# Pairwise bilinear products: the software queue's weight loads on 15 DMA engines instead of 14

## The chip, the cores and the metric

The kernel runs on one core of a Trainium2 chip. The metric is device time in microseconds (us). A core has five engines with an instruction stream each: TensorE (PE) multiplies matrices, VectorE (DVE), ScalarE (ACT) and GpSimd (POOL) work element by element, and SyncE (SP) issues transfers. Sixteen DMA engines move data between the chip's main memory (HBM) and the on-chip memory of 128 partitions. SyncE and ScalarE issue transfers on hardware queues, GpSimd on a software queue; all three queues run on the same sixteen DMA engines.

## The reference

There are 32 fields of 128 numbers for each of 1024 samples, and one 128 x 128 matrix for each of the 496 pairs (i, j) with i < j:

```python
v_i = inputs[:, I_IDX, :]
v_j = inputs[:, J_IDX, :]
transformed = jnp.einsum('bpd,ped->bpe', v_i, W)
return transformed * v_j
```

`inputs` is (1024, 32, 128), `W` is (496, 128, 128), all float32. The result, 1024 x 496 x 128 floats, is 260 MB; the inputs together are 49 MB.

## The kernel before

**Tiles.** The host lays x out as one 128 x 1024 tile for each field (embedding on the partitions, samples along the free dimension). The pairs are put in the order of falling i and numbered q = 0 to 495. The weights of eight pairs form one load of 128 partitions x 1024 floats, 512 KB. There are 62 such loads, c = 0 to 61. The output is stored transposed, in 124 tiles of four pairs (128 x 4 x 1024 floats, 2 MB each), and the host transposes back.

**Work per pair.** A step u handles half a pair, 512 samples. The first 15 pairs use one matmul a half (L237). All others split x and W into a rounded part and a rest, and use three matmuls a half: two in `first` (L240), which ScalarE then scales in place (L242), and one in `second` (L251), three steps later. VectorE multiplies the sum with the tile of field j into the output tile (L261). ScalarE rounds the weights (L142), GpSimd makes their rests (L144 to L146).

**Order.** The order of every engine's instructions is written out by the loop at the end of `tile_bilinear_pairs_kernel`. Stores go out on ScalarE's queue two steps after their last product: whole tiles of 2 MB, but tiles 72 to 80 (`HALF`) in halves of 1 MB, and the first and the last tile in smaller pieces. Output tiles rotate over three buffers and, where they are free, over the buffers of the grouped x tiles. VectorE's first product of a tile waits until the last store from its buffer has landed.

**Weight loads.** Three buffers hold weight loads. When the last split of a load is done, the loop takes the next one off `ring` and loads it into the buffer that came free, so a load is issued while the two before it in `ring` are still to be split. Loads with odd c, and the first ones, go out whole on SyncE's queue (L126). The 25 loads in `WAPART`, c = 12, 14 to 60, go out in two parts, in `load_apart`: the first `ROWS` = 8 x `NE` = 112 partitions on GpSimd's software queue (L108), the last 16 on SyncE's queue (L109). For these loads the host has reordered the first 112 rows, so that the source can be read as 14 groups (the slowest dimension, `a`) of 8 rows each; group a goes to the partitions 8a to 8a + 7.

**Marks.** After each such load, `BACK` = 3 pairs later, `move_on(2)` issues a small transfer on the software queue (L105). It writes a few rows of 64 bytes into a tile `mark` that nothing reads. With one `move_on(5)` at the first split pair (L283) and `move_on(13)` after the last load (L289), its arguments add up so that 14 + 2 = 16 for each load, and 5 + 25 x 14 + 24 x 2 + 13 = 416 = 26 x 16 for the whole kernel. The engines that a load leaves out are called spared below.

Of the kernel before, what the change touches and what calls it, by code (L numbers as in the profile page):

```python
# [30 lines left out]
XLEAD = 5  # L31

XG = 4
NE = 14
ROWS = 8 * NE
WAPART = tuple(range(12, 62, 2))
BACK = 3
# [14 lines left out]
def kernel(  # L52
# [22 lines left out]
    nc = tc.nc  # L75
# [12 lines left out]
    def load_x(f, pieces=1, eng=None):  # L88
        if f == 0:

            t = rpool.tile([P, WL, P], F32, tag="w", name="x_0").rearrange("p q e -> p (q e)")
        else:
            t = xpool.tile([P, BT], F32, tag=f"x{f}", name=f"x_{f}")
        s = BT // pieces
        for k in range(pieces):
            (eng or nc.sync).dma_start(out=t[:, k * s : (k + 1) * s], in_=xt[f, :, k * s : (k + 1) * s])
        x_sb[f] = t
# [3 lines left out]
    mark = xpool.tile([32, 16], F32, tag="mark", name="mark")  # L101

    def move_on(k):

        nc.gpsimd.dma_start(out=mark[: 2 * k], in_=xt[0, : 2 * k, :16].rearrange("(b a) n -> a b n", a=k))  # L105

    def load_apart(dst, src):
        nc.gpsimd.dma_start(out=dst[:ROWS], in_=src[:ROWS].rearrange("(b a) m n -> a b m n", a=NE))  # L108
        nc.sync.dma_start(out=dst[ROWS:], in_=src[ROWS:])  # L109
# [3 lines left out]
    def load_group(k, m):  # L113
        if m == XG - 1:
            group[k] = xpool.tile([P, XG, BT], F32, tag=f"g{k}", name=f"x_g{k}")
        f = XG * k + 1 + m
        x_sb[f] = group[k][:, m, :]
        nc.sync.dma_start(out=x_sb[f], in_=xt[f])

    def load_w(c, splits=(0, WL), eng=nc.sync):  # L120
        w_raw[c] = rpool.tile([P, WL, P], F32, tag="w", name=f"w_{c}")
        if c in WAPART:
            load_apart(w_raw[c], wt[c])
            return
        for a, b in zip(splits, splits[1:]):
            eng.dma_start(out=w_raw[c][:, a:b, :], in_=wt[c, :, a:b, :])  # L126
# [102 lines left out]
    def first(u):  # L229
        q, h = divmod(u, 2)  # L230
        i, c = pairs[q][0], q // WC
        r = slice(q % WC * P, (q % WC + 1) * P)
        s = slice(h * HB, (h + 1) * HB)
        if h == 0:
            po[q] = ppool.tile([P, BT], F32, tag="po", name=f"po_{q}")
        if q < nq0:
            nc.tensor.matmul(po[q][:, s], w_raw[q // WL][:, q % WL, :], x_sb[i][:, s], start=True, stop=True)  # L237
        else:
            for t in (0, 1):
                m = nc.tensor.matmul(po[q][:, s], w_s[c][t][:, r], x_s[i][t][:, s], start=t == 0, stop=t == 1)  # L240
                apart(m, scaled.get(u - 1) if h else None)
            scaled[u] = nc.scalar.mul(po[q][:, s], po[q][:, s], 1.0 + EPS)  # L242
            apart(scaled[u], taken.get(q - PB), "TensorE's products, which this waits for, have waited for it")

    def second(u):
        q, h = divmod(u, 2)
        i, j = pairs[q]
        r = slice(q % WC * P, (q % WC + 1) * P)
        s = slice(h * HB, (h + 1) * HB)
        if q >= nq0:  # L250
            m = nc.tensor.matmul(  # L251
                po[q][:, s], w_s[q // WC][2][:, r], x_s[i][2][:, s], start=False, stop=True, skip_group_check=True
            )
            apart(m, scaled[u ^ 1])
        g, k = divmod(q, OG)
        if k == 0 and h == 0:
            ots[g] = out_tile(g)
        if q >= NQ - 2:
            nc.vector.tensor_tensor(ots[g][:, k, s], po[q][:, s], x_sb[j][:, s], ALU.mult)  # L259
        elif h == 1:  # L260
            taken[q] = nc.vector.tensor_tensor(ots[g][:, k, :], po.pop(q), x_sb[j], ALU.mult)  # L261
            if HALF[0] < g <= HALF[-1]:
                apart(taken[q], taken.get(q - 3 * OG), "one engine writes both, in order")
        if q >= NQ - 2:
            stores.append((u + SLAG, out[g, :, k, s], ots[g][:, k, s]))
        elif g == 0 or q >= NQ - OG:
            if h == 1:
                stores.append((u + SLAG, out[g, :, k], ots[g][:, k]))
        elif g in HALF:
            if k % 2 == 1 and h == 1:  # L270
                stores.append((u + SLAG, out[g, :, k - 1 : k + 1], ots[g][:, k - 1 : k + 1]))
        elif k == OG - 1 and h == 1:
            stores.append((u + SLAG, out[g], ots[g]))

    for u in range(2 * NQ + LAG + SLAG):
        q = u // 2
        if u < 2 * NQ:
            i, j = pairs[q]
            if u % 2 == 0 and j == i + 1 and XG * ngroup < i - 2 - XLEAD:
                load_x(i - 2 - XLEAD)  # L280
            first(u)
            if u == 2 * nq0:
                move_on(5)  # L283
            if u % 2 == 0 and q in group_at:
                load_group(*group_at[q])
            if u % 2 == 1 and q in w_at:
                load_w(w_at[q])
            if u % 2 == 0 and q in back:
                move_on(16 - NE if max(w_raw) < WAPART[-1] else 13)  # L289
        if LAG <= u < 2 * NQ + LAG:  # L290
            second(u - LAG)
        while stores and stores[0][0] <= u - LAG:
            nc.scalar.dma_start(*stores.pop(0)[1:])
        if u % 2 == 1:
            ready = [t for t in todo if t[0] <= q]
            if ready:
                ready[0][2](u)
                todo.remove(ready[0])
        if ring[WB:] and ring[0] in spent:
            ring.pop(0)  # L300
            c = ring[WB - 1]
            if c == "x":
                load_x(0)
            else:
                load_w(c)
            if c in WAPART:
                back.append(q + BACK)
        while later and later[0][0] <= u:
            nc.vector.tensor_tensor(*later.pop(0)[1:], ALU.subtract)  # L309
# [31 lines left out]
```

## Time and profile before

| | |
|---|---|
| Three timed runs | 746.7, 749.0 and 752.5 us, median 749.0 |
| Profiled execution | 747.5 us, its span 745.8 us, mean granted TensorE clock 0.99 |
| TensorE matmul, weight load | 704.2 us (94%), 548.9 us (74%) busy |
| VectorE, ScalarE, GpSimd | 635.6, 635.4 and 596.8 us busy (85, 85 and 80%) |
| HBM | 49.29 MB read, 260.05 MB written, 415 GB/s over the span |
| Stores of 2 MB | 113, 13.0 us from issue to landing in the median |
| Software queue's loads of 448 KB | 25, issued from 125.5 to 683.5 us, 625 ns of GpSimd each, 11.8 us to landing |
| SyncE's parts of 64 KB | 25, issued from 124.2 to 682.3 us, 6.0 us to landing |
| SyncE's loads of 512 KB of weights | 36, 11.1 us to landing |
| Marks | 26, issued from 31.2 to 686.2 us, 634 ns of GpSimd each in the median, 10.1 us to landing |

Busy time is the time that an engine's instructions cover; it does not tell which engine is waited for. The profile also gives DMA shares: the time that packets took, as a share of what the 16 engines have. As packets on one engine overlap by some nanoseconds, a share can be a little over 1. The chain that ended last, followed back from the last instruction, is put down to TensorE for 65% of the span, to transfers for 19%, to VectorE for 7% and to GpSimd for 5%.

### The profile page before, as it was taken

To read this page: it belongs to the slowest core of one execution; us is meant where nothing else is said; L and a number is where in the kernel's file an instruction comes from. 1 tells how busy PE (TensorE), PEld (TensorE's weight loads), DVE (VectorE), ACT (ScalarE), POOL (GpSimd) and SP (SyncE) were. 2 spreads that over 40 slices of the span, in tenths; PEclk is the share of its full clock that TensorE was granted. 3 is DMA by queue.
4 is the path that set the end of the run, shared out by engine and by line. 5 is a ranking of instruction groups with operands and counts; after the bars stand their busy time and mean duration, and the time that the engine had idled before them with its cause. 6 is when DMAs were issued, how large, how long until landed. Compare 5 with 4: busy or idle time off the path is not lost.

```text
span 745.8 us, 10667 instructions
## 1 busy us (share of the span) xinstructions
PE 704.2 (94%) x2946; PEld 548.9 (74%) x2946; DVE 635.6 (85%) x550; ACT 635.4 (85%) x1256; POOL 596.8 (80%) x882
## 2 busy tenths in 40 slices
PE   7999999999999999999899979988999999999994
PEld 3577777777878887786687758866878777777783
DVE  4888999999999998887789858978988888888884
ACT  1398999999999999898899959988989989988893
POOL 1789999999999999878778857977787878796660
PEclk9999999999999999999999989999999999999997
DMA  9999999999999999999999999999999999999998
GB/s 345 426 424 428 427 428 428 425 427 421 428 419 426 426 423 426 425 422 425 427 421 430 421 423 382 417 420 431 407 423 408 422 413 418 393 407 416 423 389 342
DMA packets 35963, 310.04 MB, mean 416 GB/s; under 512 B 5440, under 2 KB 5568, under 8 KB 19136
## 3 DMA queue, kind: packets, MB, share of 16 engines
q10 hardware_dynamic: 20880, 261.10, 83.4%
q1 hardware_dynamic: 10592, 36.77, 12.3%
q0 software_dynamic: 4432, 11.48, 4.0%
q8 instruction: 24, 0.39, 0.2%
q14 instruction: 35, 0.29, 0.1%
HBM read 49.29 MB, written 260.05 MB: 415 GB/s over the span
## 4 chain that ended last, share of the span: by engine, by line
PE 65%; DMA 19%; DVE 7%; POOL 5%; issue 2%; ACT 1%; SPq 0%; DVEq 0%; POOLq 0%; ACTq 0%
PE po L240 42%; PE po L251 20%; DMA out_dram<-ot 18%; DVE ot L261 5%; PE po L237 3%; DVE xd L309 2%; POOL wd L146 1%; POOL wl L144 1%; POOL xl L161 1%; DMA x<-in_xt_dram 1%; POOL xl L162 1%; POOL wd L145 0%; ACT po L242 0%; DVE ot L259 0%; ACT wh L142 0%
## 5 line engine op out<-in xcount | busy, mean ns | idle before, releaser
L242 ACT ACTIVATE po<-po 128x512 f32<-128x512 f32 x962 | 553.6, 584 | 78.1 <-PE po L240 63.8
L261 DVE TENSOR_TENSOR ot<-po,x 128x1024 f32<-128x1024 f32 x358 | 430.1, 1221 | 70.2 <-DMA out_dram<-ot 20.9
L240 PE MATMUL po<-xh,wh 128*128 128x512 f32 x962 | 382.5, 398 | 23.0 <-DVE ot L261 22.4
L251 PE MATMUL po<-xd,wd 128*128 128x512 f32 x962 | 376.0, 391 | 4.8 <-DVE xd L309 2.4
L240 PE MATMUL po<-xl,wl 128*128 128x512 f32 x962 | 377.0, 392 | 1.5 <-POOL wl L144 0.9
L240 PEld LDWEIGHTS po<-xh,wh 128*128 128x128 f32 x962 | 181.0, 188 | 82.0 <-DVE ot L261 45.3
L144 POOL TENSOR_TENSOR wl<-w,wh 128x256 fp32r<-128x256 f32 x241 | 184.4, 765 | 66.6 <-ACT wh L142 60.8
L251 PEld LDWEIGHTS po<-xd,wd 128*128 128x128 f32 x962 | 180.9, 188 | 45.4 <-DVE ot L259 3.2
L240 PEld LDWEIGHTS po<-xl,wl 128*128 128x128 f32 x962 | 181.2, 188 | 41.3 <-POOL wl L144 4.2
L146 POOL TENSOR_TENSOR wd<-wl,wd 128x256 fp32r<-128x256 f32 x241 | 181.8, 754 | 20.1
L261 DVE TENSOR_TENSOR ot<-po,x_g 128x1024 f32<-128x1024 f32 x136 | 164.0, 1223 | 31.3 <-DMA out_dram<-ot 11.4
L145 POOL TENSOR_SCALAR wd<-wh 128x256 fp32r<-128x256 f32 x241 | 104.0, 432 | 20.5
L142 ACT ACTIVATE wh<-w 128x256 fp32r<-128x256 f32 x241 | 98.6, 410 | 7.0 <-DVE ot L261 3.6
L309 DVE TENSOR_TENSOR xd<-xh,xl 128x512 fp32r<-128x512 f32 x52 | 46.8, 901 | 0.0
L161 POOL TENSOR_TENSOR xl<-x_g,xh 128x512 fp32r<-128x512 f32 x32 | 41.7, 1302 | 4.2 <-ACT xh L160 3.9
L161 POOL TENSOR_TENSOR xl<-x,xh 128x512 fp32r<-128x512 f32 x20 | 25.9, 1293 | 15.6 <-ACT xh L160 15.3
L162 POOL TENSOR_SCALAR xl<-xl 128x512 fp32r<-128x512 f32 x52 | 34.5, 664 | 4.6
L237 PE MATMUL po<-x,w 128*128 128x512 f32 x60 | 28.1, 624 | 4.1 <-DMA x<-in_xt_dram 3.9
L237 PEld LDWEIGHTS po<-x,w 128*128 128x128 f32 x60 | 11.6, 198 | 19.8 <-issue 13.6
L160 ACT ACTIVATE xh<-x 128x512 fp32r<-128x512 f32 x20 | 12.3, 624 | 11.3 <-DMA x<-in_xt_dram 11.2
L160 ACT ACTIVATE xh<-x_g 128x512 fp32r<-128x512 f32 x32 | 20.0, 624 | 0.0
L105 POOL DMA_DIRECT2D mark<-in_xt_dram x26 | 16.6, 639 | 0.0
(7 smaller groups left out, 20.0 us busy)
## 6 DMA issues: line engine op xcount, KB each, us to landing
out_dram<-ot ACTq DMA_DIRECT2D x113, 2048.0 KB, 13.0
w<-in_wt_dram SPq DMA_DIRECT2D x36, 512.0 KB, 11.1
out_dram<-ot ACTq DMA_DIRECT2D x18, 1024.0 KB, 11.8
w<-in_wt_dram POOLq DMA_DIRECT2D x25, 448.0 KB, 11.8
x_g<-in_xt_dram SPq DMA_DIRECT2D x16, 512.0 KB, 16.4
x<-in_xt_dram SPq DMA_DIRECT2D x14, 512.0 KB, 9.5
out_dram<-ot ACTq DMA_DIRECT2D x6, 512.0 KB, 8.5
w<-in_wt_dram SPq DMA_DIRECT2D x26, 64.0 KB, 6.0
```

The costliest lines, as they stand in the source:

```text
L142: halved[c] = nc.scalar.mul(h, raw, 1.0 - 2.0**-13)
L144: nc.gpsimd.tensor_tensor(l, raw, h.bitcast(F32), ALU.subtract)
L145: nc.gpsimd.tensor_scalar(d, h.bitcast(F32), EPS, 1.0, ALU.mult, ALU.mult)
L146: nc.gpsimd.tensor_tensor(d, l.bitcast(F32), d.bitcast(F32), ALU.subtract)
L161: nc.gpsimd.tensor_tensor(l, x_sb[f][:, s], h.bitcast(F32), ALU.subtract)
L162: nc.gpsimd.tensor_scalar(l, l.bitcast(F32), 1.0 / EPS, 1.0, ALU.mult, ALU.mult)
L237: nc.tensor.matmul(po[q][:, s], w_raw[q // WL][:, q % WL, :], x_sb[i][:, s], start=True, stop=True)
L240: m = nc.tensor.matmul(po[q][:, s], w_s[c][t][:, r], x_s[i][t][:, s], start=t == 0, stop=t == 1)
L242: scaled[u] = nc.scalar.mul(po[q][:, s], po[q][:, s], 1.0 + EPS)
L251: m = nc.tensor.matmul(po[q][:, s], w_s[q // WC][2][:, r], x_s[i][2][:, s], start=False, stop=True, skip_group_check=True)
L261: taken[q] = nc.vector.tensor_tensor(ots[g][:, k, :], po.pop(q), x_sb[j], ALU.mult)
L309: nc.vector.tensor_tensor(*later.pop(0)[1:], ALU.subtract)
```

## The change

`NE` goes from 14 to 15. So a load in `WAPART` puts 120 partitions on the software queue, from a source whose slowest dimension is 15, and 8 partitions on SyncE's queue; the host reorders 120 rows to match. The mark after each load is called with 16 - 15 = 1 and becomes a transfer of a single element; the first mark is called with 4, and the last one, as before, with 13: 4 + 25 x 15 + 24 x 1 + 13 = 416 again. The spread over the ring becomes 15 engines, with one left out, and that is the fourth from where the cursor stands at the kernel's start. The halves of tiles 72 to 80 are in both kernels and are not changed.

```diff
-NE = 14
+NE = 15
 ROWS = 8 * NE
...
     def move_on(k):
 
-        nc.gpsimd.dma_start(out=mark[: 2 * k], in_=xt[0, : 2 * k, :16].rearrange("(b a) n -> a b n", a=k))
+        if k == 1:
+            nc.gpsimd.dma_start(out=mark[:1, :1], in_=xt[0, :1, :1])
+        else:
+            nc.gpsimd.dma_start(out=mark[: 2 * k], in_=xt[0, : 2 * k, :16].rearrange("(b a) n -> a b n", a=k))
...
             if u == 2 * nq0:
-                move_on(5)
+                move_on(4)
```

## The prediction

> **What bounds the kernel now.** I read the DMA part of the page first, because one row of it has no free slice:
>
> ```profile
> DMA  9999999999999999999999999999999999999998
> DMA packets 35963, 310.04 MB, mean 416 GB/s; under 512 B 5440, under 2 KB 5568, under 8 KB 19136
> ...
> q10 hardware_dynamic: 20880, 261.10, 83.4%
> q1 hardware_dynamic: 10592, 36.77, 12.3%
> q0 software_dynamic: 4432, 11.48, 4.0%
> ```
>
> The reader is to see that the queues' shares sum to about 100% of 16 engines' span: the stores (q10) take 83.4, SyncE's loads (q1) 12.3, the software queue that the change touches (q0) only 4.0. The DMA engines have no rest. Next, the busy times by stretch (columns: stretch, length, each engine's busy us with its instructions, granted clock, DMA share, GB/s); the 25 loads in question are issued between 125.5 and 683.5 us:
>
> ```profile
> 125.00:694.00 569.00, 547.01 (x2338) 435.61 (x2338) 491.68 (x426) 509.95 (x1011) 475.84 (x710) 0.99 1.01 419
> ...
> 712.00:730.00 18.00, 18.00 (x81) 14.91 (x80) 16.24 (x14) 16.62 (x33) 11.73 (x19) 1.00 0.94 400
> ```
>
> From 712 us the DMA share falls under 1 and TensorE does 81 matmuls in 18 us, 4.5 per us. In the loads' stretch it does 2338 in 569, 4.11 per us. At 4.5 it would need 519 us, so it has some 50 us of slack there, though it looks 96% busy: the DMA engines set the pace. The waits show where that enters:
>
> ```profile
> PEld po L240 <- DVE ot L261: 45.3, 59, 5.8
> DVE ot L261 <- DMA out_dram<-ot: 32.3, 35, 6.2
> ...
> ACT wh L142 <- DMA w<-in_wt_dram: 1.3, 1, 1.3
> ```
>
> VectorE waits for an output tile whose store has not landed, TensorE's weight loads then wait for VectorE; the weights themselves are waited for once, 1.3 us.
>
> A store is over when the last of the 16 engines is, so what counts is the load of each engine, which no view gives. The trace has every packet's start, length, size and queue, not its engine. But a packet starts 3 to 4 ns before the one ahead of it on its engine ends, so 16 chains can be followed, closely enough through the first nine loads. From 40 to 315 us: every chain did 420 to 428 packets of stores (all keep step), with idle gaps of a few us at most. Fourteen chains moved 7.31 to 7.38 MB, and their packets took together about 1.0 us each more than the usual durations (611 ns for 16 KB, 159 ns for 4 KB). The two spared ones, which have no 4 KB packets of the software queue, moved 7.06 and 7.07 MB, and theirs took 10.9 and 11.1 us more. One is slow steadily: from about 40 us on, 16 KB take mostly 626 to 655 ns instead of 611. The other is slow in bursts of 650 to 1208 ns, from the time at which the loads begin. Sparing took 72 packets of 159 ns, 11.4 us, from each; slowness gave 10 back. **Both spared engines are slow, and sparing them is what makes all sixteen equal.**
>
> **What the Trainium skill says.** "DMA: Bandwidth & Descriptors", section "Why a DMA increments its semaphore by 16 and not by 1": the engine count k is the largest up to 16 that divides both sides' slowest dimension; the software queue takes k consecutive engines from a cursor that goes round, a hardware queue the lowest-numbered k. The trace agrees: 66 packets of 128 B, which is 5 + 24 x 2 + 13, the marks' values of k; two chains per load carry no data; and they stay the same two, so the marks do move the cursor. The same page, section "Latency and other measured facts", calls engines 7 and 15 usually slower. Here the two slow chains both carried data of the first mark, the one of five engines, so they lie among the first five of the ring: the trace decides. Section "Queues, rings and completion order": an engine goes round its queues packet by packet. The trace agrees: the 4 KB packets of a load come mostly every 0.76 us on an engine, 611 + 159 less the overlap.
>
> **The change, part by part.** TensorE, VectorE and ScalarE issue the same instructions in the same order. POOL and SyncE issue the same number at the same places; only their shapes differ.
> (a) The load on POOL (L108 before): 120 rows on 15 engines instead of 112 on 14. The first mark now moves the cursor by 4, and 15 engines from there leave out only the fourth. The fifth, spared before, gains 8 packets of 4 KB in each of 25 loads: 200 x 159 ns = 31.8 us. It loses the 8 fillers of 4 B that a spared engine gets in their place, 200 x 9 ns = 1.8. Net **+30.0 us on that one engine**. It has no free time to hide it in: its chain is full from 40 to 315 us, and the DMA share stays at 0.99 or more until 712. The bound from below is nothing, if its slowness went away; from above, 200 x 178 ns, the longer 4 KB packets that the steadily slow chain shows, 35.6 less 1.8, so 34.
> (b) SyncE's part (L109): 8 rows instead of 16. By the skill k is then 8, the first eight engines, one row each, as now. The last eight lose 25 x 159 ns = 4.0 us each. Worth nothing: the others do not get faster, and stores wait for the slowest.
> (c) The marks: the first of 8 rows instead of 10, 24 of one element instead of four rows. A mark takes POOL 634 ns before, and the trace has none of one element. Some 0.1 us either way each, 2.4 us in all, on an engine that is 80% busy and that nothing waits for but by short waits at L240 (4.2 us). I take 0.
> (d) What is queued behind: a load's 8 packets need 5.5 us on a chain (129.8 to 135.3 us in the first), so it is not held up by the stores' backlog on that engine, since the queues take turns. Stores are late, then VectorE at L261, then TensorE.
>
> Sum: +30.0, less what the engine can catch up where it is not full. From 712 to 730 us the share is 0.94, 1.1 us idle, and about 1 of the last 16 us: **+28**. Span 745.8 + 28 = 774; the profiled execution took 747.5, and the median of three is 749.0, 1.5 above it. Forecast **777 us**, plus 3.7%.
>
> **Rivals.**
> R1, not slower: the slowness leaves the engine, because it comes of being spared, of the fillers, of a full fabric, or of being traced. Then the fifth engine becomes one of 15 equal ones, 9 rows a load as they have, and the time stays at **748 to 749**. For it: the bursts begin only with the loads. Against it: the steady one is slow from 40 us, before any load, and the bursts also hit it (388 to 390 us: 993 ns on one and 979 on the other). The slowness is 10 us in 275, some 26 to 28 us over the run, and each us that stays is one of time: it decides where under 7.5 of them stay.
> R2, the change does not do what it says: a mark of one element does not move the cursor. Each load then starts one engine earlier in the ring, the spared place goes round, and both slow engines lose nearly all their relief: 30 us less the one or two loads in which each is spared, **775 to 779**. The trace shows k of 2, 5 and 13 moving the cursor, never 1.
> R3, more than the sum: the weights come late as well, and ScalarE's split (L142), with POOL behind it, waits at each load: 1 us at 25 loads, **800**. Against it: one wait of 1.3 us in the whole run, though SyncE's loads take 11.1 us to land in the median and POOL's 11.8.
>
> **How the numbers follow.** My forecast 0.79, R1 0.09, R2 0.06, R3 0.06. Own range of the forecast: 768 (a third of the slowness gone) to 783 (long packets, 749 + 34). For 8 in 10 I go down to 762, half the slowness gone, and up to 786; R1 and R3 stay out, 0.15. About 1% (7.5 us; the three runs differ by 5.7) is what can be told from no change. Slower by more: 0.79 + 0.06 + 0.06 less 0.01 for a forecast that shrinks under it, 0.90. Within: R1's larger part and that 0.01, 0.08. Faster: 0.02, the rest of R1.
>
> **What would show it.** Right: 3,000 packets of 4 KB on q0 instead of 2,800 and 200 fewer on q1; bytes nearly the same; the DMA share down from 1.01 to about 0.97 in the loads' stretch, since fifteen engines wait for one; stores some us longer to land than 13.0; VectorE's wait for them up from 32 us to perhaps 60; TensorE's 4.11 matmuls per us down to 3.9. Wrong: the share still 1.01 with the time unchanged (R1), data missing on a different engine at each load (R2), or ScalarE waiting for weights (R3).

## The result and the profile after

The changed kernel takes **758.7 us** in the median of four runs, beside 748.1 for the kernel before on the same chip: ratio 1.0132 [1.0089, 1.0175]. It is slower, by 10 us and not by the 28 forecast, and under the whole range of 762 to 786. The profiled execution took 759.2 us, its span 757.3, which is 11.5 more than before. Lines have moved down by 3: L261 is now L264, L240 is L243, L105 is L106 (one element) and L108 (other marks).

The DMA part of the page of the changed kernel (slices of the span; then packets; then queues with packets, MB, share):

```profile
DMA  9999999999999999899999997999999999999997
...
DMA packets 35563, 310.03 MB, mean 409 GB/s; under 512 B 5040, under 2 KB 5168, under 8 KB 18736
...
q10 hardware_dynamic: 20880, 261.10, 82.1%
q1 hardware_dynamic: 10192, 35.95, 12.1%
q0 software_dynamic: 4432, 12.30, 4.6%
```

The row of nines is almost the same, but for an 8 in the 17th slice and a 7 in the 25th: about 303 to 322 and 454 to 473 us. The bytes are the same and the rate fell from 416 to 409 GB/s. The busy times by stretch of the changed kernel (stretch, length, busy us with instructions of PE, PEld, DVE, ACT, POOL, then clock, DMA share, GB/s):

```profile
125.00:694.00 569.00, 541.94 (x2300) 429.38 (x2298) 483.86 (x420) 502.97 (x994) 468.58 (x700) 0.99 1.00 412
...
712.00:730.00 18.00, 18.00 (x80) 14.73 (x80) 16.11 (x14) 16.27 (x33) 11.97 (x19) 1.00 0.97 412
```

The DMA share in the loads' stretch is 1.00 where 0.97 was forecast, and TensorE does 2300 / 569 = 4.04 matmuls per us (4.11 before, 3.9 forecast). The waits of the changed kernel (us in total, times, longest):

```profile
PEld po L243 <- DVE ot L264: 52.8, 65, 6.1
DVE ot L264 <- DMA out_dram<-ot: 49.4, 45, 6.6
PE po L243 <- DVE ot L264: 26.9, 34, 5.7
```

It is the chain of the prediction: VectorE waits for a store to land, TensorE for VectorE. VectorE's wait grew by 17 us, that of TensorE's weight loads by 7.5. That of its matmuls grew by 4.5; before, it was:

```profile
PE po L240 <- DVE ot L261: 22.4, 26, 5.4
```

Now to where in the run. Busy times of two stretches, first of the kernel before, then of the changed one:

```profile
290.00:330.00 40.00, 38.22 (x166) 30.39 (x165) 33.78 (x30) 36.04 (x72) 33.32 (x51) 1.00 1.01 426
400.00:475.00 75.00, 69.48 (x293) 55.71 (x292) 60.85 (x54) 63.13 (x127) 57.95 (x88) 0.95 1.00 411
```

```profile
290.00:330.00 40.00, 34.86 (x145) 28.01 (x144) 30.26 (x27) 31.19 (x63) 27.87 (x42) 0.91 0.95 386
400.00:475.00 75.00, 68.62 (x283) 54.01 (x282) 58.18 (x52) 61.50 (x121) 55.41 (x84) 0.95 0.94 382
```

Here, and hardly elsewhere, the engines do stand idle: TensorE does 21 and 10 matmuls fewer. VectorE's timeline of the changed kernel at the first place (start, length, idle before it and what ended it):

```profile
296.98 1.22 DVE L264 TENSOR_TENSOR ot<-po,x 128x1024 f32<-128x1024 f32 x1
304.20 1.23 DVE L264 TENSOR_TENSOR ot<-po,x 128x1024 f32<-128x1024 f32 x1 [6.00 <-DMA out_dram<-ot]
```

One wait for a store, of 6 us. In the kernel before VectorE waits at most 1.7 us at a time between 290 and 330. These two places are where output tiles lose buffers: from pair 199 and from pair 293 on, at about 300 and 440 us, one that had been lent goes back to the grouped x tiles. (One also goes at pair 121, near 190 us, and no dip is seen there; the slow engine has little lag then.) So it looks as if a store can be late for a long time without cost, as long as there are buffers to spare, and the lateness is paid when they go.

**Whose stores are late.** With the packets put into 16 chains as in the prediction, between 40 and 300 us the steadily slow engine (the fifth of the ring) did 383 packets of the stores' queue, the others about 400. Some 15 of these 17 are 16 KB, 0.61 us each, so it lags by about 9 us. Eight loads' 8 packets of 159 ns come to 10.2. Nothing of this lag is in the DMA share.

**Where 11.5 us are, in packets.** All packets' lengths together, divided by 16 engines, are 746.05 us before and 750.15 after: 4.1 us of longer packets (the loads' 4 KB went from 163 to 169 ns in the mean, while those of 16 KB stayed, 617 and 616 ns between 40 and 300 us). Of these 4.1 us, 1.2 lie between 40 and 125 us, before the first of the 25 loads; why they are longer there is not known. Time without a packet, in the mean of the engines, was 7.6 us before and 14.9 after: 7.3 more, of which 2.4 at 300 to 320 us and 4.7 at 440 to 480. 4.1 + 7.3 = 11.4 us.

### The profile page after: what moved, and what is told of

Same layout as the page of the kernel before. It is cut to its first block, busy times and chain, and to the rows that moved or that the text cites. A ratio compares the mean times of both kernels' runs of the same rounds, so it can differ in the third digit from the quotient of the medians.

```text
span 757.3 us, 10667 instructions
## 1 busy us (share of the span) xinstructions
PE 710.3 (94%) x2946; PEld 550.9 (73%) x2946; DVE 635.2 (84%) x550; ACT 636.6 (84%) x1256; POOL 595.6 (79%) x882
## 4 chain that ended last, share of the span: by engine, by line
PE 50%; DMA 32%; DVE 8%; POOL 4%; issue 3%; ACT 1%; DVEq 0%; ACTq 0%; POOLq 0%
PE po L243 32%; DMA out_dram<-ot 31%; PE po L254 15%; DVE ot L264 6%; PE po L240 4%; DVE xd L312 2%; POOL wd L149 1%; POOL wl L147 1%; ACT po L245 1%; POOL xl L164 1%; DMA x<-in_xt_dram 1%; ACT wh L145 0%; POOL wd L148 0%; DVE ot L262 0%; POOL xl L165 0%
## 5 line engine op out<-in xcount | busy, mean ns | idle before, releaser
L264 DVE TENSOR_TENSOR ot<-po,x 128x1024 f32<-128x1024 f32 x358 | 429.6, 1221 | 81.7 <-DMA out_dram<-ot 32.0
L243 PE MATMUL po<-xh,wh 128*128 128x512 f32 x962 | 384.5, 400 | 28.1 <-DVE ot L264 26.9
L243 PE MATMUL po<-xl,wl 128*128 128x512 f32 x962 | 378.1, 393 | 1.3 <-POOL wl L147 1.0
L243 PEld LDWEIGHTS po<-xh,wh 128*128 128x128 f32 x962 | 181.6, 189 | 89.8 <-DVE ot L264 52.8
L243 PEld LDWEIGHTS po<-xl,wl 128*128 128x128 f32 x962 | 181.9, 189 | 40.6 <-POOL wl L147 3.9
L264 DVE TENSOR_TENSOR ot<-po,x_g 128x1024 f32<-128x1024 f32 x136 | 163.3, 1222 | 31.1 <-DMA out_dram<-ot 17.3
L148 POOL TENSOR_SCALAR wd<-wh 128x256 fp32r<-128x256 f32 x241 | 101.9, 423 | 20.5
L240 PE MATMUL po<-x,w 128*128 128x512 f32 x60 | 30.3, 667 | 4.0 <-DMA x<-in_xt_dram 4.0
L240 PEld LDWEIGHTS po<-x,w 128*128 128x128 f32 x60 | 12.4, 212 | 21.1 <-issue 15.1
L163 ACT ACTIVATE xh<-x 128x512 fp32r<-128x512 f32 x20 | 12.3, 625 | 11.4 <-DMA x<-in_xt_dram 11.3
L111 POOL DMA_DIRECT2D w<-in_wt_dram x25 | 16.6, 663 | 0.0
## 6 DMA issues: line engine op xcount, KB each, us to landing
w<-in_wt_dram POOLq DMA_DIRECT2D x25, 480.0 KB, 11.2
```

The lines of the kernel that those rows point to most:

```text
L148: nc.gpsimd.tensor_scalar(d, h.bitcast(F32), EPS, 1.0, ALU.mult, ALU.mult)
```

## The experiments

All ratios are to the kernel before on the same chip. The experiments ran on three chips, on which the kernel before took 749.6, 749.2 and 748.5 us in the median, so a comparison of two experiments in us can be off by about 1. Diffs are against the changed kernel where nothing else is said.

**1. Does the mark of one element move the cursor? (`no_marks`)** The sizes of the software queue's packets, counted from the trace, already speak:

```
                     4 B    8 B  128 B   4 KB
before             1,216    350     66  2,800
after              1,400     15     17  3,000
no_marks             632     15     17  3,000
```

A mark of two engines leaves 14 packets of 8 B, one on each engine that it leaves out: 24 x 14 + 11 + 3 = 350. A mark of one element leaves none of 8 B, and 768 / 24 = 32 of 4 B, two on each of the sixteen chains. It goes over all sixteen. `no_marks` leaves out the 24 marks:

```diff
         if k == 1:
-            nc.gpsimd.dma_start(out=mark[:1, :1], in_=xt[0, :1, :1])
+            return
```

> The changed kernel without its 24 one-element marks. Theory S (a one-element mark does not move the cursor, so the engine that a load leaves out goes round the ring, one back at each load): the marks do nothing, so the time is that of the changed kernel, 756 to 761 us, with data missing on a different chain at each load. Theory M (the marks move the cursor as the forecast assumed, and only the fourth engine is spared): without them the spared place goes round, the fourth engine loses its relief too, and the time changes by more than 5 us against 758.7.

Measured: 758.4 us, 1.0135 [1.0103, 1.0166]. Same time, and in the chains the same picture in both kernels: the chain without data is another one at each load, eight different ones in the changed kernel's first eight loads (131 to 294 us). **The 24 marks don't move the cursor; the spared place goes round**, which is R2. The Trainium skill ("DMA: Bandwidth & Descriptors", section "Why a DMA increments its semaphore by 16 and not by 1") has a one-element transfer on one engine, but also says that the software queue spreads some copies over 16 engines in an exception, and that only a spread over fewer than 16 goes by the cursor. The trace puts the one-element transfer among these exceptions.

**2. Are the spared engines slow, or slow because spared? (`tenth_eleventh`)** Against the kernel before, other engines are spared:

```diff
-                move_on(5)
+                move_on(11)
...
-                move_on(16 - NE if max(w_raw) < WAPART[-1] else 13)
+                move_on(16 - NE if max(w_raw) < WAPART[-1] else 7)
```

> The kernel before with its two spared engines moved: first mark 11 instead of 5, last mark 7 instead of 13, so that the tenth and the eleventh of the ring are left out. If bursts come of being spared, the fourth loses its bursts and the tenth or eleventh gets some; if they belong to the fourth, it keeps them while it carries all loads. The steadily slow chain carries all loads in either case and falls behind. Theory of sparing: 755 to 765 us. Theory that both are slow by themselves: both fall behind by 30 us of work, and the time is at least that of the changed kernel, 759 to 778 us.

Measured: 760.8 us, 1.0169 [1.0137, 1.0201]. Between 175 and 240 us the bursts (16 KB packets of 650 to 1258 ns) are on the two chains now spared, with 4.6 and 3.6 us in excess. Taken load by load, over the 18 us from its start, a chain that the load leaves out has 0.8 us of such bursts in this kernel and a chain that carries it 0.2, whichever engines they are. The time, 760.8, lies in both expected ranges and does not decide. And in the changed kernel, where no engine is spared for long, no chain has more than 2.1 us of bursts from 130 to 300 us. **The bursts of the fourth are an effect of being spared**: about 1.2 us a load, as much as the sparing took away (8 packets of 159 ns). An engine that is spared while the others carry a load has its packets stretched here, and no gaps between them; why is not known. The slowness of the fifth is still there with no relief at all (16 KB mostly 626 to 655 ns, mean 637 against 611 to 616).

**3. Sparing exactly one engine (`fourth_only`, `fifth_only`, then `fourth_only_2`, `fifth_only_2`).** Two marks of 8 and 9 engines move the cursor by 17, which is 1 in a ring of 16. `fourth_only`:

```diff
         if k == 1:
-            nc.gpsimd.dma_start(out=mark[:1, :1], in_=xt[0, :1, :1])
+            move_on(8)
+            move_on(9)
```

`fifth_only` also has 5 for the 4 of the first mark and 12 for the 13 of the last.

> The changed kernel with two marks after each load, of 8 and of 9 engines, which together move the cursor by 17, that is by 1. Theory S: only now is the fourth engine alone spared; the load's data are missing on one and the same chain throughout, the slow bursts come back on that chain, as in the kernel before, and the steadily slow fifth engine keeps all 25 loads: 760 us or more, up to the 777 of the forecast. Theory M: it spares the same engine as the changed kernel, so 757 to 761 us.

> As the kernel that spares the fourth engine alone, but with the first mark of 5 and the last of 12, so that the fifth engine alone is spared. If the steadily slow chain is the fifth engine and the bursts on the other come of its being spared (theory S with bursts from sparing): the steady one has its relief, the fourth is an engine as others, no chain shows bursts, 743 to 750 us, the kernel before or a little less. If both engines are slow by themselves, as the forecast had it: 757 us or more, since the fourth has lost its relief.

Measured: 889.0 us, 1.1882 [1.1836, 1.1927], and 891.0 us, 1.1918 [1.1865, 1.1971]. Both tell nothing of the engines, and the waits of `fourth_only` show why:

```profile
POOL mark L109 <- DMA mark<-in_xt_dram: 159.3, 23, 10.8
```

The second mark writes the same tile, so GpSimd waits for the first to land, 23 times some 7 us, with its weight splits queued behind it. The same two, with a tile for each mark:

```diff
+    mark2 = xpool.tile([32, 16], F32, tag="mark2", name="mark2")
...
-    def move_on(k):
+    def move_on(k, mark=mark):
...
-            nc.gpsimd.dma_start(out=mark[:1, :1], in_=xt[0, :1, :1])
+            move_on(8)
+            move_on(9, mark2)
```

> The fourth engine alone spared, again with marks of 8 and 9 engines after each load, now into two tiles, so that the second does not wait for the first on GpSimd. Theory S: data missing on one and the same chain, slow bursts on that chain, the steadily slow chain with all 25 loads as in the changed kernel: 756 to 777 us; near 759 if buffers take up the lag, near 777 if it counts in full. Theory M (the changed kernel already spares the fourth alone): 757 to 761 us and no other difference.

> The fifth engine alone spared, marks of 8 and 9 into two tiles. If the steadily slow chain is the fifth engine and bursts come of being spared: the steady chain keeps step, the bursts show on it or on none, the fourth is as the others; 743 to 750 us. If the fourth is slow by itself: 757 us or more.

Measured: `fourth_only_2` 760.4 us, 1.0164 [1.0124, 1.0205]; `fifth_only_2` **745.7 us, 0.9955 [0.9937, 0.9972]**, faster than both kernels. VectorE's wait for stores in the two, first `fourth_only_2`, then `fifth_only_2` (L266 is their L261):

```profile
DVE ot L266 <- DMA out_dram<-ot: 47.4, 42, 6.6
```

```profile
DVE ot L266 <- DMA out_dram<-ot: 28.5, 28, 5.9
```

Moving the relief from the fourth engine to the fifth is worth 15 us. On the fourth it is worth nothing (its bursts come back: 6.3 us from 128 to 300). The two kernels issue as many marks and loads at the same places, so neither the marks nor GpSimd's time for them can be the cause. Of `fifth_only_2`, the two stretches from above are full again:

```profile
290.00:330.00 40.00, 40.00 (x176) 32.61 (x176) 36.85 (x33) 37.88 (x77) 36.80 (x57) 1.00 1.01 426
400.00:475.00 75.00, 69.50 (x294) 55.92 (x293) 62.10 (x53) 63.13 (x127) 59.28 (x90) 0.95 0.99 413
```

So the change as described, with only the fourth spared, would have been as slow as the kernel that it became.

**4. No sparing, and no software queue (`all_16`, `no_software`).** `all_16` loads whole on the software queue, without SyncE's part and without the marks after loads; the host's order of rows follows:

```diff
-        nc.gpsimd.dma_start(out=dst[:ROWS], in_=src[:ROWS].rearrange("(b a) m n -> a b m n", a=NE))
-        nc.sync.dma_start(out=dst[ROWS:], in_=src[ROWS:])
+        nc.gpsimd.dma_start(out=dst, in_=src)
```

> No engine spared: whole loads of 128 partitions on the software queue, nothing on SyncE's, no marks after loads. If the changed kernel in effect spares no engine in particular, this is the same but for a sixteenth of relief on each: 757 to 763 us, one steadily slow chain that falls behind, no bursts on any. If both the fourth and the fifth are slow by themselves: 770 us or more.

Measured: 754.3 us, 1.0076 [1.0047, 1.0105], some 3 us less than expected, and less than the changed kernel, which spares an engine at each load: there SyncE's 8 rows give a ninth row to eight engines, the slow one among them (in the changed kernel's trace, the slow chain has a single 4 KB row of SyncE's 16 times beside 24 whole loads; the others together 175 beside 546). `no_software` is the kernel before with all weights on SyncE's queue:

```diff
-WAPART = tuple(range(12, 62, 2))
+WAPART = ()
```

and no mark at all.

> All weight loads whole on SyncE's queue, no software queue and no marks at all; eight rows per engine as with all sixteen. If the fifth engine's steady slowness has nothing to do with the software queue: one chain with 16 KB packets of 626 to 655 ns from about 40 us on, 752 to 757 us. If the software queue causes it: no such chain, 744 to 748 us.

Measured: 754.4 us, 1.0077 [1.0048, 1.0106]. The same time. Counted as above, the slow chain did 394 packets of the stores' queue, the others 400 to 406. The Trainium skill (same page, "Latency and other measured facts") calls two engines usually slower and guesses that it comes of the software queue. One engine is slow here, and **it is so without that queue**; which of the sixteen it is by number, and why it is slow, stays open.

**5. Is the lag paid where buffers go? (`buffers_earlier`)** `OWAIT` says how many pairs before the load of a group the output tiles stop taking its buffer. With 60 they lose the last two at pairs 159 and 253, and two earlier ones sooner too:

```diff
-OWAIT = 20
+OWAIT = 60
```

> The changed kernel with OWAIT 60 instead of 20: the output tiles lose the buffers of the grouped x tiles 40 pairs earlier, at pairs 159 and 253 instead of 199 and 293 (about 240 and 380 us instead of 300 and 440). If the lag of the slow engine is taken up by the store buffers and shows only where they become fewer: the two stretches of idle DMA engines move to about 240 and 380 us, the first one smaller since the lag is then smaller, and the time is within 5 us of 758.7. If the idle stretches have another cause, the x loads for one, they stay at 300 and 440 us.

Measured: 759.7 us, 1.0151 [1.0117, 1.0185]. Two stretches of it, and the second of the changed kernel:

```profile
290.00:330.00 40.00, 39.52 (x170) 31.16 (x170) 35.03 (x32) 36.80 (x73) 32.31 (x50) 1.00 1.01 418
...
396.00:416.00 20.00, 14.15 (x53) 11.12 (x52) 11.00 (x11) 11.09 (x23) 9.65 (x16) 0.83 0.69 289
```

```profile
396.00:416.00 20.00, 19.63 (x84) 15.43 (x84) 17.67 (x18) 18.40 (x37) 17.73 (x26) 1.00 1.01 417
```

The dip at 300 us is gone; in its place the engines stand idle for 6.4 us between 400 and 420. All idle time, 14.5 us, is that of the changed kernel (14.9). It moved later than expected and to one place, not to two; at pair 159, near 240 us, nothing is seen. But the place moved and the sum did not, so in this pair of kernels **the buffers decide where the lag is paid, not how much**.

**6. How much relief, and when? (`relief_early_4`, `relief_late_4`, `relief_9`)** These are `fifth_only_2` with relief in only some of the 25 loads; the others go out whole, over all 16, without marks. `SPARE` is `WAPART[:4]`, `WAPART[-4:]` or `WAPART[::3]`:

```diff
+SPARE = WAPART[:4]
...
-    def load_apart(dst, src):
+    def load_apart(dst, src, c):
+        if c not in SPARE:
+            nc.gpsimd.dma_start(out=dst, in_=src)
+            return
```

> All sixteen engines carry the software queue's loads, as in the kernel without a spared engine (754.3 us), but the fifth is spared in the first four of the 25. Theory W (the slow fifth engine's whole work sets the end): each spared load takes 8 x 155 ns from it and adds one row of SyncE's, 1.1 us; four give 750 us, early or late. Theory B (its lag costs only where the output tiles lose buffers, at about 300 and 440 us): four early ones take half of the lag at 300 us away and make the first idle stretch vanish, 749 to 752 us.

> The same with the fifth engine spared in the last four loads, after 590 us. Theory W: 750 us, as with four early ones. Theory B: after 475 us no engine idles, so relief there is worth nothing or only what the tail gives back, 752.5 to 754.5 us.

> The fifth engine spared in every third load, nine of 25; else all sixteen. Theory W: 754.3 less 9.8 us, but not under what else limits the kernel, which the kernel that always spares the fifth shows at 745.7: 744 to 747 us. Theory B: much the same, 745 to 749, since lag is taken off before both steps.

Measured: first four loads 751.9 us, 1.0029 [1.0014, 1.0044]; last four 750.6, 1.0035 [1.0019, 1.0051]; every third load, nine in all, **745.65, 0.9961 [0.9945, 0.9977]**. Late relief is worth all that theory W gave it (750) and more than B allowed (752.5 to 754.5); early relief comes out 2 us short of W's 750. The ratios' intervals overlap, though the medians are 1.3 us apart. So, to within these 2 us, it is the whole work of the slow engine that counts, not its lag at one place. And nine loads do what 25 do. `relief_9` and `fifth_only_2` are the fastest; their intervals overlap.

**The sum that fits.** Take the work of the slow engine at its own pace, an estimate from the trace's durations less 4 ns of overlap, without the packets of 4 and 8 B (under 2 us). Stores and the small x loads are 904 packets of 607 ns, 144 of 305, 48 of 155, 64 of 80: 605.2 us. The other loads are 92 x 8 packets of 155: 114.1. Instruction fetches, 0.3% of the span: 2.3. Its slowness is 25 ns on each of 904 packets: 22.6. That makes 744.2 with 8 rows in each load. A ninth row in 25 loads adds 3.9; a spared load takes off 7 rows, 1.1. Beside it the measured spans:

```
kernel                              work of the fifth   span           span less work
fourth_only_2, tenth_eleventh       748.1               758.3, 759.0   10.2, 10.9
after (spared once or twice)        746 to 747          757.3          10 to 11
all_16, no_software                 744.2               752.6, 752.7   8.4, 8.5
four loads relieved, early, late    739.9               748.7, 748.6   8.8, 8.7
relief_9                            734.4               743.6          9.2
before                              717                 745.8          29
fifth_only_2                        717                 743.2          26
```

The spans are those of the profiled executions; that of the four early loads is the fastest of its twenty, 1.4 us under the median. Down to `relief_9` the span follows the fifth's work at 8 to 11 us; W's times for the three kernels with part of the relief were forecast before they ran. From there to 717 nothing is gained: something else holds the span at 743 to 746. It is not the work of a normal engine alone, which is 744.2 - 22.6 + 3.9 = 725.5 with nine rows. What it is has not been tried.

## Why the prediction was wrong

**The step that failed is (a)'s "It has no free time to hide it in: its chain is full from 40 to 315 us, and the DMA share stays at 0.99 or more until 712."** A chain full over the first nine loads was taken to be full of work in the whole run. Up to 315 us it nearly was: the packets of the spared slow chain took some 0.9 us a load more than the usual durations, and its own pace, 25 ns on some 32 packets of 16 KB, is 0.8 of that. After 315 us it was not. Packets of 4 KB and more took 9.7 us more than the usual durations on the average engine from 315 to 694 us, where from 40 to 315 it was 2.5. Where the slow chain can still be told apart after 379 us, it is mostly 1.3 to 2.5 us a load over. Stretched packets keep both the chain and the share full, so the room did not show as idle time. In the kernel before, the fifth had 717 us of work in a span of 745.8, and its relief was more than it needed: `relief_9` shows that nine relieved loads in 25 are enough. Of the 30 us that the fifth got back, 11.5 came out in the span; by the sum above the other 18.5 filled room that was there. The stretching of its packets that could be followed makes up some 10 of these, by estimate; where the rest lay isn't shown. In the forecast the term "+30.0, less what the engine can catch up" was mis-sized in its second half: 18.5, not 2.

- **"Both spared engines are slow, and sparing them is what makes all sixteen equal"** is half right. The fifth is slow by itself. The fourth was slow because it was spared, which R1 held for both. The trace had the sign, and the prediction named it: its bursts begin with the loads. But R1's time, 748 to 749, did not come, since the fifth's slowness stayed.
- **(a), the mechanism**: R2 is what happened, with a chance of 0.06. The 4 KB packets are 3,000, as forecast, and the spared place goes round, so it is not "only the fourth" that is left out, as the change and the forecast have it. That the forecast had the direction right in spite of this is in part luck: the fifth loses its relief either way. The wrong place made little of the error: `fourth_only_2`, where the fourth is really spared, is at 1.0164 [1.0124, 1.0205]. R2's own price, 775 to 779, had the same term in it.
- **(b)** was not tried by itself. The slow engine is among the first eight and has its row of SyncE's part in both kernels, so nothing was to be gained there.
- **(c)** holds: a one-element mark took GpSimd 605 ns instead of 634, and without the 24 marks the time is the same.
- **(d)** holds: the stores were late and the loads were not (11.2 us to landing, 11.8 before), so R3 did not come.
- **What would show it**: VectorE's wait 49 us where "perhaps 60" was said, 4.04 matmuls per us for 3.9. The first went 17 of its 28 us, the second a third of its way. The share of 0.97 did not come. The idle time of the waiting engines was in two places of some 20 and 40 us, with stretched packets elsewhere.

## What to carry to other kernels

A DMA engine that is busy to the last slice may still have room: compare its work at the usual packet durations, not its busy time, with the span, and over the whole run, not over its first part. When the relief of one engine is to be sized, try half of it and none of it; the value of more ends at a knee, here at about nine loads in 25. And count the small packets before trusting that a small transfer takes the engines that its shape suggests.

## What was not expected of the hardware

- The stretched packets: about 1.2 us in excess per load on whichever steady engine was spared. On the slow one, when spared, there is hardly any beyond its own pace before 315 us.
- One of the sixteen DMA engines takes 637 ns for 16 KB where the others take 611 to 616, in every kernel looked at, the one without a software queue among them, and on each of the three chips of the experiments. Sparing the fifth of the ring relieves it on two of them (`fifth_only_2` and `relief_9`).
- During a wait of 5 us TensorE's clock was halved. TensorE's timeline of the changed kernel (start, length, idle before):

```profile
305.48 0.79 PE L243 MATMUL po<-xh,wh 128*128 128x512 f32 x1 [5.14 <-DVE ot L264]
306.07 0.63 PE L243 MATMUL po<-xl,wl 128*128 128x512 f32 x1
306.50 0.63 PE L254 MATMUL po<-xd,wd 128*128 128x512 f32 x1
```

Matmuls of 0.63 us stand where 0.39 is usual; the clock was low for 6.8 us, from 302.3. The Trainium skill ("TensorE: Matmul & The Clock Gate", section "What's actually happening") lets an idle window of about 3.4 us halve the clock and a busy one restore it. The trace agrees that it is halved and restored, but not on a whole idle window: the last matmul had ended at 300.3, so the clock fell after 2.0 us of idle time. Ahead of the tail it happens twice in the changed kernel (again at 452.5, after 4.5 us) and once before (at 440.7, after 2.9), so a late store costs TensorE a little more than the wait.
